# Stores of the attention's numerators and denominators: from SP's queue to ScalarE's, early in the next slot

## The chip, the cores and the metric

The kernel runs on one core of a Trainium2 chip. A core has five engines, each with its own stream of instructions that it works through in order: PE (TensorE, matrix products, with its weight loads shown as PEld), DVE (VectorE), ACT (ScalarE), POOL (GpSimd) and SP (SyncE, which here does nothing but issue DMA transfers). The engines wait for each other through semaphores. A DMA is started by an instruction on one engine's queue and then moves its data by itself. The metric is the device time of one execution in microseconds; the median of the runs is what counts.

## What is computed

The reference is one transformer layer on 4096 tokens of width 512, in 32-bit floats. The attention is linear and causal: a running state takes in one token after the other.

```python
q = elu(rope(x @ Wq.T)) + 1          # 16 heads of 128
k = elu(rope(x @ Wk.T)) + 1          # 4 heads, each used by 4 query heads
v = x @ Wv.T                          # 4 heads
state, z = state + outer(k_s, v_s), z + k_s
num = einsum('bhe,bhed->bhd', q_s, state)
den = einsum('bhe,bhe->bh', q_s, z) + EPS
attn = (num / den) @ Wo.T
x = layernorm(x + attn)
x = layernorm(x + ffn(x))             # Walsh-Hadamard transforms, 2 x 2048 inner columns, SiLU gate
```

The change touches how `num` and `den` leave the core.

## The kernel before

**Stages.** The attention comes first (about 43 to 910 us of the profiled execution), then the output product with Wo and the first layernorm, then the feed-forward part. Every factor of a product is split into a rounded high part and a remainder (`xh` and `xl`, `qh` and `ql`, `sh` and `sl`), and each product is made of three matrix products, which gives nearly full 32-bit precision.

**Blocks and slots.** The tokens are cut into `NB = 16` blocks of 256. The attention goes over them twice, since the weights of two of the four key heads fit at a time: pass 0 does key heads 0 and 1, pass 1 the heads 2 and 3. That makes 32 block steps `n`. A block step has four slots, `(g, p)` with key head `g` of the pass and half `p` of the block: 128 slots in all, one round of the loop over `slots` each. In each slot PE does 24 matmuls of a projection some slots ahead (`proj_q`), shares of the projections of keys and values of the block after (`proj_k`, `proj_v`), the transposes and sums of the running state (`nat_k`, `state`), the scores inside a chunk of 64 tokens (`scores`), and `av`, which brings all together.

**What `av` does.** For the head's half block it sums state times queries and values times scores in `ps_num` (L443), and the denominators of four query heads in `ps_den` (L444). ScalarE copies `ps_num` to the tile `num` (L447; three buffers), and the copy is stored to `num_d` in device memory (L449), 256 KB. After the second half (`p == 1`) ScalarE copies the denominators to `ds` (L452; one buffer), and two stores of 2 KB take them to `den_d` (L453 to 455). `num_d` and `den_d` are read again later: the denominators by `recip_load`, one block at a time, during the second pass and after; the numerators in the stage after, and some already in the last slots.

**The other work of the engines in a slot.** `rope` (L294 to 304) turns projections into rotated features: two copies on ScalarE to `sw`, a product on GpSimd (L296), one on VectorE (L297), a sum (L300), an exponential on ScalarE (L301), and a last step on VectorE (L304). `proj_q` splits the result into `qh` (ScalarE, L395) and `ql` (VectorE, L397). `scores` makes `A` from `ps_sc` with ScalarE (L416), VectorE (`am` L419, `A` L420) and GpSimd (L423); `ps_sc` has one buffer in PSUM.

**SP's queue.** Each DMA of the kernel is issued by `dma()` at L58, on SP. In the attention these are, besides the stores of numerators and denominators: the loads of x (`raw`, or `xh` and `xl` in the second pass, from `xs_d`), of weights, of the table of cosines (`csb`); and per block the transfers of shifted values, which lay `vhl` one token later into the tiles `vst` (three or four transfers) and `vd` (four). The state's matmul (L366) reads `vst`, and `av` reads `vd`. Sums of feed-forward weights for later (`wsum`, `was_d`) go through the same queue.

**What sets the order.** The kernel is written against a tile framework, whose planner takes the whole program and sets the order of each engine's stream from its own costs of each instruction; what is marked with `pin` keeps its place in program order. So the engines' streams are fixed before the run, and a change of one instruction's engine can reorder the rest. A tile pool with `bufs=n` hands out n buffers in turn; who takes one waits until the last use of its earlier content is over. The completion semaphores of DMAs are eight, given out in turn over all DMAs of all queues; a DMA waits until the one eight places before it has landed.

Of the kernel before, what the change touches and what calls it, by code (L numbers as in the profile page):

```python
# [43 lines left out]
def kernel(  # L44
# [5 lines left out]
    nc = tc.nc  # L50
    V, S, G, T = nc.vector, nc.scalar, nc.gpsimd, nc.tensor

    def dma(dst, src, pin=False):
        if dst.dtype == F32R:
            dst = dst.bitcast(F32)
        if src.dtype == F32R:
            src = src.bitcast(F32)
        i = nc.sync.dma_start(dst, src)  # L58
        if pin:
            tc.keep_in_program_order(i)  # L60

# [6 lines left out]
    num_d = [dram.tile([128, KVH, 512], F32, name=f"num_d{t}") for t in range(32)]  # L68
    den_d = [dram.tile([KVH, 4, 2, 64], F32, name=f"den_d{t}") for t in range(32)]
# [17 lines left out]
    def load_raw(src):  # L87
        pool, tag, nb = first.pop(0) if first else (praw, "raw", 3)
        raw = pool.tile([128, 512], F32, tag=tag, name="raw", bufs=nb)
        dma(raw, src)  # L90
        return raw
# [19 lines left out]
    def wo_raw(h, raw):  # L111
        WR[h] = raw
        dma(raw, wo[h], True)

    def wo_split(eng, *hs):
        for h in hs:
            if h < NH - 4:
                hi, lo = (wres.tile([128, 512], F32R, tag="w", name=x) for x in ("wh", "wl"))
            else:
                w = late["p"].tile([128, 2, 512], F32R, tag="wx", name="wx", bufs=4)  # L120
                hi, lo = w[:, 0], w[:, 1]
                if h == NH - 1:
                    late["p"].tile([128, 8], F32, tag="edge", name="edge", bufs=1)
            hilo(hi, lo, WR.pop(h), eng, True)
            WO[h] = (hi, lo)
# [3 lines left out]
    def recip_load(b):  # L129
        dn = pout.tile([128, 2, 16], F32, tag="dn", name="dn", bufs=2)  # L130
        for j in range(2):
            dma(dn[:, j], den_d[2 * b + j].rearrange("g h c q -> (g h c q)").rearrange("(p n) -> p n", p=128), True)
        return b, dn

    def recip(b, dn):
        pin(V.reciprocal(dn, dn))
        for j in range(2):
            dma(rec_d[2 * b + j].rearrange("(p n) -> p n", p=128), dn[:, j])
# [41 lines left out]
    with ExitStack() as es:  # L180
# [109 lines left out]
        def rope(ps, csb, f, stay=False):  # L290
            cosb = csb[:, 0:1].to_broadcast([128, 2, 256])
            sinb = csb[:, 1:2].to_broadcast([128, 2, 256])
            sw = pe.tile([128, 2, 256], F32, tag="sw", name="sw", bufs=3)
            S.activation(sw[0:64], ps[64:128], AF.Copy)  # L294
            S.activation(sw[64:128], ps[0:64], AF.Copy)  # L295
            G.tensor_tensor(sw, sw, sinb, ALU.mult)  # L296
            V.tensor_tensor(ps, ps, cosb, ALU.mult)  # L297
            yield
            x1 = ps if stay else pe.tile([128, 2, 256], F32, tag="x1", name="x1", bufs=2)
            V.scalar_tensor_tensor(x1, ps, 1.0, sw, ALU.add, ALU.add)  # L300
            S.activation(sw, x1, AF.Exp, bias=neg1)  # L301
            yield
            f = (ps if stay else sw) if f is None else f
            V.scalar_tensor_tensor(f, sw, 1.0, x1, ALU.min, ALU.max)  # L304
            return f

        def proj(n, keys):
            B = blk[n]
            ps = pmm.tile([128, 2, 256], F32, tag="mm", name="ps_qk")
            for j, key in enumerate(keys):  # L310
                i = 0
                for k in range(4):
                    for wa, xa in ((0, "xh"), (0, "xl"), (1, "xh")):
                        T.matmul(ps[:, j], W[key][wa][:, k * 128:(k + 1) * 128], B[xa][:, k],  # L314
                                 start=i == 0, stop=i == 11)
                        i += 1
            return ps
# [68 lines left out]
        def proj_q(j):  # L386
            n, g, hp = j // 4, j // 2 % 2, j % 2
            s, b = divmod(n, NB)
            B = blk[n]
            ps = proj(n, [("q", s, g, 2 * hp), ("q", s, g, 2 * hp + 1)])  # L390
            f = yield from rope(ps, B["csb"], None, hp == 1)
            if hp == 0:
                B["q", g] = tuple(p3.tile([128, 4, 256], F32R, tag=t, name=t, bufs=4) for t in ("qh", "ql"))
            qh, ql = (a[:, 2 * hp:2 * hp + 2] for a in B["q", g])
            S.activation(qh, f, AF.Copy)  # L395
            yield
            V.tensor_tensor(ql, f, qh.bitcast(F32), ALU.subtract)  # L397
# [28 lines left out]
        def av(n, g, p):  # L426
            s, b = divmod(n, NB)
            B = blk[n]
            A = B.pop(("A", g, p))
            qh, ql = B["q", g]  # L430
            sh, sl, _ = B["S"][g]
            gs = slice(g * 128, (g + 1) * 128)
            if p == 0:
                B["den", g] = pden.tile([4, 256], F32, tag="den", name="ps_den")
            den = B["den", g]
            ps = pnum.tile([128, 2, 256], F32, tag="num", name="ps_num")
            for c2 in range(2):
                c = 2 * p + c2
                t = slice(64 * c, 64 * c + 64)
                ops = [(sh[:, c], qh[:, :, t]), (sh[:, c], ql[:, :, t]), (sl[:, c], qh[:, :, t]),  # L440
                       (B["vd"][:, c, 0, gs], A[:, c2]), (B["vd"][:, c, 1, gs], A[:, c2])]
                for i, (l, r) in enumerate(ops):
                    T.matmul(ps[:, c2], l, r, start=i == 0, stop=i == len(ops) - 1)  # L443
                T.matmul(den, selr[:, c], A[:, c2], start=c == 0, stop=c == 3)  # L444
            gg = 2 * s + g
            num = p3.tile([128, 4, 2, 64], F32, tag="num", name="num", bufs=3)
            S.activation(num.rearrange("p h c q -> p c h q"),  # L447
                         ps.rearrange("p c (h q) -> p c h q", h=4), AF.Copy)
            dma(num_d[2 * b + p][:, gg], num.rearrange("p h c q -> p (h c q)"))  # L449
            if p == 1:  # L450
                ds = pout.tile([4, 256], F32, tag="ds", name="ds", bufs=1)
                S.activation(ds, den, AF.Copy, bias=EPS_DEN)  # L452
                for j in range(2):  # L453
                    dma(den_d[2 * b + j][gg].rearrange("h c q -> c h q"),
                        ds[2 * j:2 * j + 2].rearrange("c (h q) -> c h q", h=4))

        def wcomb(p):
            r = {}
# [14 lines left out]
        def wcomb_all():  # L473
            for p in range(8):
                yield from wcomb(p)
                yield
                yield
# [56 lines left out]
        def go(gen):  # L534
            if gen is not None:
                next(gen, None)
# [14 lines left out]
        for j in range(2):  # L551
            c = slice(j * 512, (j + 1) * 512)
# [9 lines left out]
        nsc = SA  # L562
        gw = wcomb_all()
        gk = gs1 = gv = None
        for i, (n, g, p) in enumerate(slots):
            nxt = n + 1 < N
            sl = (g, p)
# [11 lines left out]
                go(gk)  # L579
            if sl == (1, 0):  # L580
                go(gk)
            gq2 = proj_q(i + QA) if i + QA < NQ else None
            go(gq2)
            if sl == (0, 0):
# [40 lines left out]
            elif sl == (1, 1):  # L625
                go(gs1)
                if n == N - 2:
                    gs2 = state(N - 1, 1)
                    go(gs2)
            av(n, g, p)  # L630
            if sl == (0, 1) or n == N - 2:
                go(gv)
# [63 lines left out]
            if sl == (1, 1):  # L696
                if "dn" in cur:
                    recip(*cur.pop("dn"))
                if NB + LAG <= n < N - 4 + LAG:
                    cur["dn"] = recip_load(n - NB - LAG)  # L700
                blk.pop(n - 1, None)

        wo_split(V, 11)
        wo_split(G, 12)
# [340 lines left out]
    with ExitStack() as es:  # L1045
# [23 lines left out]
        for n in range(NS):  # L1069
            f, p = divmod(n, 8)  # L1070
            bank, sv, c = {}, {}, {}
# [13 lines left out]
            for s, tag in enumerate(SEQ):  # L1085
# [3 lines left out]
                for u in (1, 0):  # L1089
# [3 lines left out]
                    i = 0  # L1093
# [11 lines left out]
                    if s in (1, 4, 6):  # L1105
                        src, k, q = {1: (ps, 0, 0), 4: (bank.get(("b", u)), 4, 3), 6: (ps, 2, 1)}[s]
# [68 lines left out]
    with ExitStack() as es:  # L1175
# [53 lines left out]
        for idx, (n, s) in enumerate(order):  # L1229
# [40 lines left out]
            i = 0  # L1270
# [98 lines left out]
```

## Time and profile before

| what | value |
|---|---|
| median of 3 runs | 2250.24 us (2250.07 to 2251.79) |
| profiled execution, its own time | 2251.69 us |
| its span | 2250.0 us |
| granted TensorE clock, mean | 0.991 |
| PE busy over the span | 2190.9 us, 97% |
| DVE busy | 1742.0 us, 77% |
| ACT busy | 1376.5 us, 61% |
| POOL busy | 1294.6 us, 58% |
| DMA queue of SP | 501.19 MB, 69.7% of 16 engines' span |
| attention stage, 40 to 910 us: DVE, ACT busy | 761.50 and 634.49 of 870 us |

How to read it. "Busy" is the time that an engine spends on its operations; an engine that issues DMAs is not counted busy for that. Matmuls overlap in the array, so PE's busy time counts more than the time between their starts, and PE at 97% may still stand for some 2 us here and there. A wait is given as `engine line <- engine tile line: us, times, longest`: who waited, for what, in all. A line of the timeline gives start, duration, engine, operation, and in brackets how long the engine was idle just before and what ended it. The chain that ended last is followed back from the last instruction of the run, so its shares say which engine the end depended on.

### The profile page before, as it was taken

The numbers are of one execution on the slowest core, as the hardware profiler recorded it, in microseconds if no ns is written. First come the engines' busy times: TensorE is split into PE (matmuls) and PEld (weight loads), VectorE is DVE, ScalarE is ACT, GpSimd is POOL, SyncE is SP. The second block draws the span as 40 slices with busy tenths as digits, with TensorE's granted clock in tenths as the row PEclk, the third lists the DMA queues.
The fourth block names the chain that finished last, engine by engine and source line by source line (L and its number), as shares of the span: only waits on it lengthen the run. The fifth ranks groups of instructions, "written<-read, shape, count | busy, mean of one in ns | idle before, by whom it ended". The sixth has DMA issues, their size and how long they took to land.

```text
span 2250.0 us, 42158 instructions
## 1 busy us (share of the span) xinstructions
PE 2190.9 (97%) x14319; PEld 1989.9 (88%) x14319; DVE 1742.0 (77%) x2690; ACT 1376.5 (61%) x2490; POOL 1294.6 (58%) x1089
## 2 busy tenths in 40 slices
PE   8999999899999999999999999999999999999998
PEld 8999999899999998788888778778888888999998
DVE  8999998888888888688898766766866765665655
ACT  8777776677777776444443466655655655554553
POOL 5666665555555556377887446565555555533332
PEclk9999999999999999999999999999999999999999
DMA  6666665555666666889998876876766767886673
GB/s 223 204 211 197 224 218 174 164 173 181 191 199 185 199 182 198 317 264 280 296 275 276 285 262 218 249 235 193 240 211 195 244 196 213 280 287 217 228 247 128
DMA packets 360121, 503.88 MB, mean 224 GB/s; under 512 B 67964, under 2 KB 187004, under 8 KB 355938
## 3 DMA queue, kind: packets, MB, share of 16 engines
q1 hardware_dynamic: 359906, 501.19, 69.7%
q8 instruction: 113, 1.85, 0.3%
q14 instruction: 102, 0.84, 0.1%
HBM read 282.76 MB, written 156.76 MB: 195 GB/s over the span
## 4 chain that ended last, share of the span: by engine, by line
PE 62%; DVE 15%; DMA 7%; ACT 6%; issue 4%; SPq 3%; POOL 2%; DVEq 0%; POOLq 0%; ACTq 0%
PE ps_a L1096 14%; PE ps_wo L174 11%; PE ps_da L1276 8%; PE ps_b L1096 7%; PE ps_qk L314 5%; PE ps_db L1276 4%; PE ps_c L1096 3%; SPq L58 3%; DVE ps_qk L297 2%; PE ps_v L263 2%; PE ps_dc L1276 2%; PE ps_num L443 2%; DMA vst<-vhl 2%; DVE am L419 2%; DVE ql L397 1%
## 5 line engine op out<-in xcount | busy, mean ns | idle before, releaser
L314 PE MATMUL ps_qk<-xh,wh 128*128 128x256 f32 x1280 | 357.7, 279 | 1.2 <-DVE x L300 0.8
L314 PE MATMUL ps_qk<-xl,wh 128*128 128x256 f32 x1280 | 356.9, 279 | 0.0
L314 PE MATMUL ps_qk<-xh,wl 128*128 128x256 f32 x1280 | 356.7, 279 | 0.0
L1078 POOL TENSOR_TENSOR cc<-cc 128x512 f32<-128x512 f32 x96 | 146.4, 1528 | 274.9 <-ACT cc L1075 130.5
L95 DVE TENSOR_TENSOR wol<-A,woh 128x512 fp32r<-128x512 f32 x217 | 222.3, 1031 | 95.8 <-ACT woh L94 84.4
L296 POOL TENSOR_TENSOR sw<-sw,csb 128x512 f32<-128x512 f32 x160 | 212.3, 1327 | 134.7 <-ACT sw L295 118.7
L423 POOL TENSOR_SCALAR_AFFINE_SELECT A<-A 64x512 fp32r<-64x512 f32 x256 | 196.0, 766 | 144.4 <-DVE am L419 92.1
L314 PEld LDWEIGHTS ps_qk<-xh,wh 128*128 128x128 f32 x1280 | 242.3, 189 | 5.5 <-DVE ql L397 1.4
L314 PEld LDWEIGHTS ps_qk<-xl,wh 128*128 128x128 f32 x1280 | 241.2, 188 | 0.9
L314 PEld LDWEIGHTS ps_qk<-xh,wl 128*128 128x128 f32 x1280 | 241.3, 189 | 0.7
L94 ACT ACTIVATE woh<-A 128x512 fp32r<-128x512 f32 x217 | 135.1, 628 | 124.6 <-PE ps_b L1096 72.7
L94 ACT ACTIVATE hah<-hraw 128x512 fp32r<-128x512 f32 x212 | 132.1, 629 | 123.8 <-PE ps_da L1276 65.2
L95 POOL TENSOR_TENSOR hal<-hraw,hah 128x512 fp32r<-128x512 f32 x74 | 98.6, 1332 | 188.8 <-PE ps_da L1276 82.2
L1096 PE MATMUL ps_a<-yoh,woh 128*128 128x512 f32 x512 | 200.5, 393 | 5.8 <-ACT sv L1103 5.2
L1096 PE MATMUL ps_a<-yol,woh 128*128 128x512 f32 x512 | 200.1, 391 | 0.0
L1096 PE MATMUL ps_a<-yoh,wol 128*128 128x512 f32 x512 | 197.2, 391 | 0.0
L95 DVE TENSOR_TENSOR hal<-hraw,hah 128x512 fp32r<-128x512 f32 x138 | 99.0, 723 | 106.5 <-PE ps_da L1276 40.3
L1103 ACT ACTIVATE sv<-ps_a,wsc 128x512 f32<-128x512 f32 x192 | 127.0, 680 | 35.0 <-PE ps_a L1096 34.7
L174 PE MATMUL ps_wo<-wh,oh 128*128 128x512 f32 x368 | 144.5, 393 | 0.0
L174 PE MATMUL ps_wo<-wl,oh 128*128 128x512 f32 x368 | 144.0, 391 | 0.0
L174 PE MATMUL ps_wo<-wh,ol 128*128 128x512 f32 x368 | 143.9, 391 | 0.0
L297 DVE TENSOR_TENSOR ps_qk<-ps_qk,csb 128x512 f32<-128x512 f32 x160 | 111.3, 696 | 40.6 <-ACT sw L295 39.3
(306 smaller groups left out, 7312.3 us busy)
## 6 DMA issues: line engine op xcount, KB each, us to landing
hraw<-hop_d SPq DMA_DIRECT2D x224, 256.0 KB
num_d<-num SPq DMA_DIRECT2D x128, 256.0 KB
rb<-rec_d SPq DMA_DIRECT2D x128, 256.0 KB
hop_d<-hS SPq DMA_DIRECT2D x128, 256.0 KB
vd<-vhl SPq DMA_DIRECT2D x128, 252.0 KB
nt<-num_d SPq DMA_DIRECT2D x31, 1024.0 KB
A<-in_wug_dram SPq DMA_DIRECT2D x93, 256.0 KB
hop_d<-cc SPq DMA_DIRECT2D x64, 256.0 KB
```

The lines of the kernel that those rows point to most:

```text
L58: i = nc.sync.dma_start(dst, src)
L94: i = S.activation(hi, src, AF.Copy)
L95: j = eng.tensor_tensor(lo, src, hi.bitcast(F32), ALU.subtract)
L174: T.matmul(ps, l[:, h], r, start=i == 0, stop=i == 47)
L296: G.tensor_tensor(sw, sw, sinb, ALU.mult)
L297: V.tensor_tensor(ps, ps, cosb, ALU.mult)
L314: T.matmul(ps[:, j], W[key][wa][:, k * 128:(k + 1) * 128], B[xa][:, k], start=i == 0, stop=i == 11)
L423: G.affine_select(ah, ah.bitcast(F32), pattern=[[0, 8], [1, 64]], compare_op=ALU.is_ge, fill=0.0, base=0, channel_multiplier=-1)
L1078: G.tensor_tensor(x, x, c.pop(("g", q)), ALU.mult)
L1096: T.matmul(ps, w[:, u, k], y[:, k], start=first and i == 0, stop=i == 5, skip_group_check=not first)
L1103: S.activation(x, ps, AF.Copy, scale=sc)
L1276: T.matmul(pj[j], ops[qd][al][:, r, js], BW[s][bl][ip], start=first and (i == 0 or i == 3 and pj is ps), stop=i >= 45 or last and i == 23, ...
```

## The change

`dma()` gets an argument for the issuing engine. `av` no longer stores at once: it puts the store of `num`, and for the second half the two stores of `ds`, as functions on a list `puts`. The loop over the slots empties the list in the next slot, after that slot's first steps of `gq` and `gk` (a projection's and a key rope's next part) and before `proj_q` of the slot, and issues the stores on ScalarE's queue. After the last slot the list is emptied once more. 256 of the kernel's 2090 DMAs move: 128 of 256 KB and 128 of 2 KB.

```diff
-    def dma(dst, src, pin=False):
+    def dma(dst, src, pin=False, eng=nc.sync):
...
-        i = nc.sync.dma_start(dst, src)
+        i = eng.dma_start(dst, src)
...
             S.activation(num.rearrange("p h c q -> p c h q"),
                          ps.rearrange("p c (h q) -> p c h q", h=4), AF.Copy)
-            dma(num_d[2 * b + p][:, gg], num.rearrange("p h c q -> p (h c q)"))
+            puts.append(lambda: dma(num_d[2 * b + p][:, gg], num.rearrange("p h c q -> p (h c q)"), eng=S))
             if p == 1:
                 ds = pout.tile([4, 256], F32, tag="ds", name="ds", bufs=1)
                 S.activation(ds, den, AF.Copy, bias=EPS_DEN)
                 for j in range(2):
-                    dma(den_d[2 * b + j][gg].rearrange("h c q -> c h q"),
-                        ds[2 * j:2 * j + 2].rearrange("c (h q) -> c h q", h=4))
+                    puts.append(lambda j=j: dma(den_d[2 * b + j][gg].rearrange("h c q -> c h q"),
+                                                ds[2 * j:2 * j + 2].rearrange("c (h q) -> c h q", h=4), eng=S))
...
         gk = gs1 = gv = None
+        puts = []
         for i, (n, g, p) in enumerate(slots):
...
             if sl == (1, 0):
                 go(gk)
+            while puts:
+                puts.pop(0)()
             gq2 = proj_q(i + QA) if i + QA < NQ else None
...
                 blk.pop(n - 1, None)
+        while puts:
+            puts.pop(0)()
```

## The prediction

> **What bounds the kernel now.** I read the busy table first, then the attention stage alone (40 to 910 us; the changed lines run nowhere else), then what PE and SP wait for there, then single stalls. The page:
>
> ```profile
> PE 2190.9 (97%) x14319; PEld 1989.9 (88%) x14319; DVE 1742.0 (77%) x2690; ACT 1376.5 (61%) x2490; POOL 1294.6 (58%) x1089
> ...
> PE 62%; DVE 15%; DMA 7%; ACT 6%; issue 4%; SPq 3%; POOL 2%; DVEq 0%; POOLq 0%; ACTq 0%
> ...
> q1 hardware_dynamic: 359906, 501.19, 69.7%
> ```
>
> and the table by stretch (from:to and length, then busy time and count of PE, PEld, DVE, ACT and POOL, then granted clock, DMA share, GB/s):
>
> ```profile
> 40.00:910.00 870.00, 835.57 (x6967) 815.49 (x6966) 761.50 (x1222) 634.49 (x1176) 530.00 (x533) 0.98 0.61 193
> ```
>
> PE is the bound. A block of 256 tokens has 4 slots of 56 matmuls, which start 0.117 us apart when nothing is in the way, so 32 blocks need 32 x 224 x 0.117 = 839 us of the some 867 that they take. No change to queues can win more than about 28 us, and anything that makes PE pause costs in full. DVE is 88% busy beside it, ACT 73%. Next the waits of SP and PE in the stage (us in all, times, longest):
>
> ```profile
> SPq L58 <- ACT num L447: 58.6, 26, 5.9
> SPq L58 <- ACT ds L452: 25.6, 9, 6.7
> SPq L58 <- DMA xh<-xs_d: 18.6, 28, 2.0
> ```
>
> ```profile
> PE ps_sc L409 <- DVE A L420: 9.2, 3, 5.1
> PE ps_v L263 <- DVE ql L397: 8.4, 6, 4.4
> PE ps_s L366 <- DMA vst<-vhl: 7.1, 13, 1.2
> ```
>
> Two kinds of stall in them matter. The first kind recurs in blocks of the second pass: the state matmul (L366) waits for the stores of the shifted values, which SP issues among the stores of the change. SP's queue, and PE just after it:
>
> ```profile
> 607.02 0.88 SPq L58 DMA_DIRECT2D vst<-vhl  x1
> 608.00 0.48 SPq L58 DMA_DIRECT2D num_d<-num  x1
> 608.58 1.33 SPq L58 DMA_DIRECT2D den_d<-ds  x2
> 609.96 1.54 SPq L58 DMA_DIRECT2D vst<-vhl  x2
> ```
>
> ```profile
> 614.22 0.62 PE L366 MATMUL ps_s<-vst,kfn 128*128 128x256 f32 x3 [0.61 <-DMA vst<-vhl]
> ```
>
> The second is DVE's order. At 126.33 PE stands 0.98 us for a ql, because seven DVE instructions of two ropes, a state sum and the score correction stand close together:
>
> ```profile
> 126.33 0.39 PE L263 MATMUL ps_v<-wh,xh 128*128 128x256 f32 x1 [0.98 <-DVE ql L397]
> ```
>
> One stall at the end of the stage hangs on the stores as well: the num copy waits for an earlier num_d store, queued behind some 3 MB of loads, and with it the weights behind it on ACT and PE (4.83 us idle at 909.34, and half clock for some us after).
>
> ```profile
> 907.92 0.60 ACT L447 ACTIVATE num<-ps_num 128x512 f32<-128x512 f32 x1 [6.05 <-DMA num_d<-num]
> ```
>
> **The change, part by part.** The sum is made against the profiled run's own 2251.69 us (span 2250.0, 1.69 around it), 1.45 above the median of 2250.24; I add the sum to the median.
>
> *Taken from SP.* 256 issues. One num_d issue takes 425 ns at the median, one den_d issue 268 (the longest 2003 and 1459), by these rows:
>
> ```profile
> L58 SPq DMA_DIRECT2D num_d<-num x128: 319/425/2003, 43.9 to 908.5; - x128
> L58 SPq DMA_DIRECT2D den_d<-ds x128: 234/268/1459, 51.1 to 909.3; - x128
> ```
>
> At the medians that is 128 x 0.425 + 128 x 0.268 = 88.7 us; added up over the trace it is 78.2 + 49.7 = 127.9 us. SP is no bound, and its 84.2 us of waits for num and ds cost something only where a transfer behind them is late. Three such places:
> - Second pass, vst: 7.1 us over 13 waits. In the built order of the changed kernel the last vst store stands 20 to 24 matmuls before the state matmul instead of 16, 0.5 to 0.9 us more, and num_d and den_d are gone from between. Bounds 0 and -7.1; I take -5.
> - Pass change (361 to 440 us): ACT stands 3.95 us for a wv load that SP issued late, PE 4.44 us after it. The load's own landing, 4.4 us from issue, stays. Bounds 0 and -7, I take -3.
> - End of the stage: bounds +5 and -6. ACT's last stores now wait themselves for SP's 1 MB loads of numerators, but the num copy can start earlier. I take -3.
>
> Sum of gains: -11.
>
> *Added to ACT.* The same 256 issues, now between its activations, at the same duration (the nearest row, since ACT issues nothing before): 88.7 to 127.9 us on top of 634.49 of 870, from 73% to 83 to 88% busy. What hides it is ACT's 235 us idle in the stage. What is behind an issue on ACT is the rope's sw copies, exps and qh, and DVE and POOL already wait for the sw copies (38.5 us in 53 waits of DVE, 117.6 us in 79 of POOL). Bounds: 0 if all fall into idle time, +128 if all lie on the path. Between them I go by the chain that ended last: ACT has 6% of 2250 us on it, 135 of its 1376.5 busy us, so a tenth of its work counts. A tenth of 89 to 128 is 9 to 13; I take +10.
>
> *Waits that ACT now holds.* In the built program each DMA waits for the landing of the DMA eight before it, of either queue. 224 of ACT's 256 stores carry such a wait, 158 of them for a transfer of SP's; most lie 40 to 60 matmuls (5 to 7 us) behind it, and a vst transfer lands in 3.49 us in the chain of waits. SP's waits of this sort are 18.6 us for xh, and 9.2 for xl. Bounds: 0 if all have landed, +28 if ACT took them all over and on the path. A quarter of them, 7 us, at a tenth: +1. The store's wait for its own num or ds costs nothing: it is issued a slot (some 6.7 us) after the copy, num's three buffers cover a store that is one slot late, and ds, with one buffer, is written again only two slots on.
>
> *The order of all the rest.* The planner orders every engine's stream anew, and this I hold for the largest term. I counted DVE instructions per seven successive matmuls in both built programs (matmuls 400 to 7300). Places with five or more: 6 before, 40 after, with up to nine; between matmuls 400 and 3480 they are 2 before, 27 after, about two per block of the first pass; from 3481 to 7000 0 before, 9 after. A DVE instruction of these takes 0.68 us (the am row and its neighbours at 125.00: 0.67 to 0.70), so six take 4.1 us while seven matmuls need 0.8; what hides it is only what DVE runs ahead. The trace prices it: of the 11 places with four in the first pass, five held PE up by 0.79 to 1.14 us, 0.95 in the mean (a sixth by 0.57, five not). Bounds: below, 0, or -5 if these five stalls go (an order for SP's sake can also be the better one); above, 36 x 1.9 = +68 if each costs twice what a place with four does. I take 25 new ones in the first pass at 0.95 less the 4.8 lost there already, = +19, and the 9 of the second pass at half of it, as DVE has lighter stretches around them, = +4: +23, of which the +10 for ACT's issues pays for part (the same pause is not lost twice); for the overlap I take off 3.
>
> Sum: -11 + 10 + 1 + 23 - 3 = +20, so 2251.69 + 20 = 2271.7 for the profiled run, 2250.24 + 20 = 2270 for the median.
>
> One rule weighed here: the Trainium skill, DMA: Bandwidth & Descriptors, section "Issuing engines are not separate DMA queues", says that DMAs of scalar, sync and gpsimd run on the same 16 engines and interleave, so that another issuing engine saves only the time of initiating. It speaks against a gain beyond SP's issue time; the trace has all transfers at 61% of the DMA engines' time in the stage, which agrees that they are not the bound. By the rule alone the gain would be the vst share, -5, and the sum +26.
>
> **Rivals.** *Faster (2230 to 2244, middle 2238).* ACT's idle 235 us swallow the issues, the new order runs ahead of its bunches, and the gains stand: -11 to -12. For it: in the trace ACT's median instruction starts 1.5 us before the matmul that stands at its place in the built order, and 5 of 11 places with four cost nothing. Against: 27 bunches where there were 2. It decides if the mean price of a bunch is under some 0.2 us.
>
> *Within 0.2% (2246 to 2254).* 0.2% (4.5 us) is about what a measurement of this kernel can tell from no change. Gains and losses cancel, price of a bunch about 0.3 us, ACT's issues hidden.
>
> *Much slower (2286 to 2320).* An issue on ACT takes not 0.425 and 0.268 us but what SP's slow ones do when many descriptors are being made at once: vd's mean is 1.00 us. At 1.0 for num_d and 0.6 for den_d it is 205 us, ACT is 96% busy and becomes the bound beside DVE: a third of it on the path is +45 more with the order's cost, 2295 or above. Against: most of the stores stand in slots with no burst.
>
> **How the numbers follow.** Forecast (likeliest) 0.46, own range 2256 to 2286; faster 0.26; within 0.2% 0.09; much slower 0.19. So faster 0.26, same 0.09, slower 0.65. For 8 in 10 I leave out the better half of the faster case (below 2237, 0.11) and the upper part of the worst (above 2300, 0.09): 2237 to 2300. Predicted: 2270.
>
> **What would show it.** Right: num_d and den_d rows under ACT's queue at 0.3 to 0.5 us; ACT's stretch 40 to 910 at 720 to 760 us with its issues; the stage 20 us longer; "PE ps_v <- DVE ql", "PE ps_sc <- DVE A" or "PE ps_qk <- DVE" up from 20 us to 40 or more, spread over the first pass, twice a block; "PE ps_s <- DMA vst" under 3 us; the 6.05 us of the num copy gone. Wrong: if PE's waits for DVE are no longer than before, the order does not cost and the time falls to 2238; if ACT itself is what DVE and PE wait for, or its stores wait for landings, the worst case holds. Least sure is the price of a bunch, since the trace of before holds so few.

## The result and the profile after

The changed kernel takes 2350.04 us in the median of four runs (2341.46 to 2355.72) against 2250.76 us of the kernel before: a ratio of 1.0437 (95% interval 1.0399 to 1.0476), 99 us slower. The forecast was 2270 us with a range up to 2300. The direction came out as forecast, but by luck: the term that gave the forecast its sign is not the one that costs. The size did not: the loss is five times what was forecast, and the experiments below show that it comes from a term that the prediction had put at 1 us. One execution among those of the experiments, 2384.57 us at a granted clock of 0.849 in the run with the first head's stores on ACT, is left out of that run's ratio.

The page of the changed kernel's profiled execution (span 2353.0 us):

```profile
PE 2228.9 (95%) x14319; PEld 2017.0 (86%) x14319; DVE 1750.5 (74%) x2690; ACT 1371.3 (58%) x2490; POOL 1297.9 (55%) x1089
...
q1 hardware_dynamic: 340194, 467.36, 63.4%
q10 hardware_dynamic: 19712, 33.83, 4.2%
...
PE 59%; DMA 13%; DVE 10%; ACT 6%; POOL 5%; issue 4%; SPq 3%; ACTq 1%; DVEq 0%; POOLq 0%
```

A second queue, q10, now carries the stores. ACT is no busier in operations than before (its issues are not counted as busy), and in the chain that ended last it is not ACT that has grown but DMA, from 7% to 13%, and POOL, from 2% to 5%. The stage (the table by stretch, columns as before) now ends about 102 us later:

```profile
40.00:1012.00 972.00, 875.31 (x6968) 845.33 (x6966) 763.67 (x1221) 628.45 (x1174) 527.38 (x532) 0.95 0.56 172
```

The same number of matmuls as before takes 972 us in place of 870, at a granted clock of 0.95 in place of 0.98. I added up the pauses of PE from the start times of its matmuls: every interval of more than 0.35 us, less the 0.117 us of an undisturbed one. Between matmuls 400 and 2900 (first pass) they were 5.6 us before and are 37.9 now, between 3480 and 7000 (second pass) 10.6 and 51.5. Together that is 73 us more of standing; the rest of the two passes' +102 us is matmuls that start more slowly, nearly all of them within 8 us after a pause. The stages behind the attention take as long as before (1325.6 and 1325.4 us from matmul 7240 on).

PE's waits in the first 1030 us (us in all, times, longest) name ACT first:

```profile
PE ps_num L443 <- ACT num L447: 39.6, 18, 5.9
PE ps_sc L409 <- DVE A L420: 14.9, 14, 3.3
PE ps_num L443 <- ACT sh L382: 11.6, 6, 4.1
...
PE ps_s L366 <- DMA vst<-vhl: 0.9, 2, 0.7
```

The last line was 7.1 us before, and the first was this:

```profile
PE ps_num L443 <- ACT num L447: 1.0, 1, 1.0
```

So the hoped-for gain is there: the stores of the shifted values are no longer waited for. And a new wait is there that is far larger. Where it comes from is seen on ACT, here in the timeline of the changed kernel (idle time just before an instruction, and what ended it, in brackets):

```profile
245.81 0.36 ACT L452 ACTIVATE ds<-ps_den 4x256 f32<-4x256 f32 x1
250.30 0.37 ACTq L58 DMA_DIRECT2D num_d<-num  x1
251.76 0.85 ACTq L58 DMA_DIRECT2D den_d<-ds  x2
252.66 0.69 ACT L301 ACTIVATE sw<-ps_qk,neg 128x512 f32<-128x512 f32 x1 [6.49 <-DMA xs_d<-xh]
```

and on SP, DVE and PE in the same microseconds:

```profile
241.92 4.50 SPq L58 DMA_DIRECT2D wsum<-in_wug_dram  x4
246.52 0.55 SPq L58 DMA_DIRECT2D xs_d<-xh  x1
247.15 0.38 SPq L58 DMA_DIRECT2D xs_d<-xl  x1
247.59 0.49 SPq L58 DMA_DIRECT2D xs_d<-xh  x1
```

```profile
253.38 0.70 DVE L304 SCALAR_TENSOR_TENSOR ps_qk<-sw,ps_qk 128x512 f32<-128x512 f32 x1 [4.65 <-ACT sw L301]
```

```profile
257.24 0.58 PE L443 MATMUL ps_num<-qh,sh 128*128 128x256 f32 x1 [4.51 <-ACT num L447]
257.62 0.41 PE L443 MATMUL ps_num<-ql,sh 128*128 128x256 f32 x1
```

ACT is done at 246.17 and could go on with the rope. Its next instruction is the store of num, and in the built program that store waits for the transfer eight places earlier: xs_d<-xh, which SP issues only at 246.52, since it was late with the wsum loads. ACT issues its store at 250.30, 3.78 us after that, and the two small stores behind it wait for the next xs_d transfers in the same way. In all, 6.49 us without an operation on ACT. DVE gets no rope in that time (4.65 us idle), the num copy behind it is late, and PE stands 4.51 us for a free ps_num. After the pause its matmuls take 0.41 us in place of 0.28 and start 0.21 us apart.

I call the time between the end of ACT's previous instruction and the issue of a store a *stand*. In the changed kernel 58 stores stand for more than 0.3 us, 92.8 us in all (counted as in the table below; 32 of them over 1 us). In each of the 58 the store waits on one of the eight completion semaphores, the one that it will count up itself. For all but 1.2 us of this time the awaited transfer had been issued already, 3.3 to 9.7 us before the store, and had not landed; 89.3 of the 92.8 us go to transfers that SP had issued.

### The profile page after: what moved, and what is told of

The parts are those of the page before. It is cut to its first block, busy times and chain, and to the rows that moved or that the text cites. A ratio compares the mean times of both kernels' runs of the same rounds, so it can differ in the third digit from the quotient of the medians.

```text
span 2353.0 us, 42056 instructions
## 1 busy us (share of the span) xinstructions
PE 2228.9 (95%) x14319; PEld 2017.0 (86%) x14319; DVE 1750.5 (74%) x2690; ACT 1371.3 (58%) x2490; POOL 1297.9 (55%) x1089
## 4 chain that ended last, share of the span: by engine, by line
PE 59%; DMA 13%; DVE 10%; ACT 6%; POOL 5%; issue 4%; SPq 3%; ACTq 1%; DVEq 0%; POOLq 0%
PE ps_a L1101 13%; PE ps_da L1281 7%; PE ps_qk L314 7%; PE ps_b L1101 7%; PE ps_wo L174 5%; PE ps_v L263 4%; PE ps_db L1281 4%; PE ps_c L1101 3%; SPq L58 3%; PE ps_num L443 3%; DMA rb<-rec_d 2%; PE ps_dc L1281 2%; DMA yraw<-yq_d 1%; DMA vd<-vhl 1%; DMA xs_d<-xh 1%
## 5 line engine op out<-in xcount | busy, mean ns | idle before, releaser
L294 ACT ACTIVATE sw<-ps_qk 64x512 f32<-64x512 f32 x160 | 95.3, 596 | 117.2 <-PE ps_qk L314 45.0
```

## The experiments

Three theories were to be told apart. W: ACT stands at its stores for transfers that have not landed. O: the planner's new order costs, the largest term of the prediction. I: the issue time on ACT costs. To separate order from queue I fixed the order by hand: a list of one built program's order is turned into ordering edges (no semaphores) in another.

```diff
+def _force(tc):
...
+    for e, steps in want.items():
...
+            if prev is not None:
+                tc.add_manual_dep(got[e][at], prev.name, nosync, reason="order")
+            prev = got[e][at]
```

It covers all matmuls, all instructions of DVE, ACT and POOL, and SP's transfers other than the stores; the stores are placed by the planner. In the traces of the runs with a fixed order the sequences of PE, DVE, ACT, POOL and SP's other transfers are those of the kernel that gave the order, without one exception. Each ratio below is against executions of the kernel before in the same session, whose median lay between 2246.91 and 2250.67 us.

**The changed kernel's order with the stores on SP.**

```diff
-            puts.append(lambda: dma(num_d[2 * b + p][:, gg], num.rearrange("p h c q -> p (h c q)"), eng=S))
+            puts.append(lambda: dma(num_d[2 * b + p][:, gg], num.rearrange("p h c q -> p (h c q)"), eng=nc.sync))
```

(and the same for the denominators, with the changed kernel's order fixed)

> The order of the matmuls, of DVE, ACT and POOL and of SP's other transfers is that of the changed kernel, fixed by hand; the 256 stores stand one slot late, but on SP's queue. Theory W (ACT stands at its stores until an earlier transfer has landed; in the changed kernel 63 such stands of over 0.3 us, 96 us in all): no stands are left, the time falls back to 2250 to 2265 us. Theory O (the planner's new order, the term of +23 in the prediction, is what costs): the time stays at 2320 to 2350. A mixture gives the share of each.

Measured: 2263.78 us, ratio 1.007 (1.0046 to 1.0094). PE's pauses are 6.8 us in the first pass and 12.6 in the second, nearly those of before. The order that I had held for the main cost runs at almost full speed once the stores are off ACT. Theory O falls as the main cause. 14 us stay, and what they are made of is only known in part: 8.8 us of ACT's waits are for its one `ds` buffer, which the deferral on SP holds longer (below).

**The order of before with the stores on ACT**, one slot late as in the changed kernel.

> The counterpart: the order of all compute and of SP's other transfers is that of before, fixed by hand; the 256 stores stand one slot late on ACT's queue. Theory W: ACT's idle time just before its stores is 80 to 110 us in all and the time is 2320 to 2350. Theory O: the time is 2250 to 2265, and any stands of ACT lie in time that it had spare. Theory I (the issue time on ACT, some 80 us by the rows of the changed kernel, costs and not the stands): 2270 to 2290 with few stands.

Measured: 2320.65 us, ratio 1.032 (1.0298 to 1.0342); 41 stands of over 0.3 us, 75.4 us in all; PE's pauses 18.1 and 47.8 us. So most of the loss comes with the queue, in an order that is good on SP. Theory W holds, with the time at the lower end of what it gave and the stands a little under it.

Of these 75 us the second head's stores had 72: what stands between them and the first head's is the block's burst of transfers for vst and vd and what follows it on SP. This allows the sharpest test, each half of the stores alone.

**Only the first head's stores on ACT**, the order of before:

```diff
+            put = puts.append if g == 0 else lambda f: f()
+            eng = S if g == 0 else nc.sync
-            dma(num_d[2 * b + p][:, gg], num.rearrange("p h c q -> p (h c q)"))
+            put(lambda: dma(num_d[2 * b + p][:, gg], num.rearrange("p h c q -> p (h c q)"), eng=eng))
```

> Only the stores of a block's first head (g = 0) go to ACT's queue in the next slot; those of the second stay on SP as before; the order of all compute and of SP's other transfers is that of before, fixed by hand. In the run with all stores on ACT in this order, the first head's stores (64 of num and 64 of den in a pass's terms, half of the issue time) had 4 us of stands, the second head's 73 us, since these follow a block's burst of eight transfers of shifted values. Theory W (stands): within 10 us of before, 2245 to 2262, stands under 10 us. Theory I (issue time on ACT, half of some 107 us here): about half of that run's +71, 2280 to 2290.

Measured: 2251.36 us, ratio 1.0003 (0.9989 to 1.0016), 13.3 us of stands (a little over what theory W gave), 58.2 us of issue time on ACT.

**Only the second head's stores on ACT** (`g == 1` in the same lines):

> The other half: only the stores of the second head (g = 1) on ACT, the order of before. Theory W: nearly the whole loss, 2300 to 2325, with 60 us or more of stands. Theory I: as the first half, 2280 to 2290.

Measured: 2348.84 us, ratio 1.0443 (1.0395 to 1.0491), 81.7 us of stands with only 40.6 us of issue time. The time is above what theory W gave (2300 to 2325) and far above theory I. Half of the stores cost nothing, the other half cost as much as the whole change. The half with more issue time on ACT is the free one. Lines of ACT in this run, each just behind one or more stands, which are part of its idle time:

```profile
608.21 0.59 ACT L297 ACTIVATE sw<-ps_qk 64x512 f32<-64x512 f32 x1 [1.91 <-DMA vd<-vhl]
611.67 0.63 ACT L398 ACTIVATE qh<-sw 128x512 fp32r<-128x512 f32 x1 [2.27 <-DMA wsum<-in_wug_dram]
641.44 0.59 ACT L297 ACTIVATE sw<-ps_qk 64x512 f32<-64x512 f32 x1 [4.62 <-DMA den_d<-ds]
```

These two also settle theory O's measure, which was a count of places with five or more DVE instructions within seven matmuls: the kernel before had 6 such places; with each engine's order the same as there, the built program of the free half has 62, that of the dear half 22. So the count is no property of an engine's order, and it does not foretell the time. Why the second half alone loses 28 us more than both halves together is not settled; its stands are 6 us longer in all, and its second pass has 14 us more of pauses.

**The issue time alone.** The stores stay on SP as before; ACT gets 256 small copies of some 0.41 us in their places, which write to a tile that nobody reads.

```diff
+        def spend():
+            i = S.activation(junk, ones4[:, 0:1].to_broadcast([128, 256]), AF.Copy)
...
+            puts.append(spend)
```

> The stores stay on SP as before; in their places early in the next slot ACT gets 256 small copies of a constant into a tile that nobody reads, some 0.4 us each, about the 105 us that the issues take it in the changed kernel, and they wait for nothing. The order of all else is that of before. Theory W: under +15, 2250 to 2265. Theory I: 2290 to 2320.

Measured: 2267.62 us, ratio 1.0084 (1.0061 to 1.0108). That is 3 us above what theory W gave, but it was not the dose I meant: since a copy of a constant waits for nothing, the planner put all 256 ahead, between 5.0 and 347.7 us. So I repeated it with copies that read the slot's `num` and can't be moved ahead.

```diff
-            i = S.activation(junk, ones4[:, 0:1].to_broadcast([128, 256]), AF.Copy)
+            i = S.activation(junk, num.rearrange("p h c q -> p (h c q)")[:, 0:256], AF.Copy)
```

> As the run with 256 small copies on ACT, but each copy reads the slot's num tile, so that it can't be moved ahead: in the other run the planner had put all of them into the first 348 us. In the built program they stand evenly through the stage, 256 x some 0.41 us = 105 us, as much as the changed kernel's issues take, and wait for no transfer. Order of all else as before. Theory W: 2250 to 2268. Theory I: 2290 to 2320.

Measured: 2255.73 us, ratio 1.0028 (1.0013 to 1.0043), some 6 us. The copies' row of that run, and its stage:

```profile
L432 ACT ACTIVATE junk<-num x256: 399/408/428, 45.2 to 916.0; 128x256 bf16<-128x256 f32 x128
```

```profile
40.00:920.00 880.00, 838.90 (x6985) 816.20 (x6984) 763.35 (x1227) 719.71 (x1436) 532.47 (x535) 0.99 0.60 191
```

ACT is 82% busy here and PE hardly notices. 104 us of ACT's time, about the 105 us that the changed kernel's issues take it, cost some 6 us if nothing waits in them. Theory I is bounded by that.

**A queue without the shared semaphores.** The changed kernel with `eng=G`, POOL's queue:

> As the changed kernel, but the stores are issued on POOL's queue, whose transfers have completion semaphores of their own, so that in the built program not one of the 256 stores waits for a transfer's landing. Theory W: 2245 to 2275, since POOL is only 61% busy in the stage. Theory O: the planner bunches here too (15 places with five DVE instructions in seven matmuls, against 6 and 40), so about a quarter of the loss, 2270 to 2285. If an issue on a computing engine costs in itself: 2290 or more.

Measured: 2272.22 us, ratio 1.0107 (1.0078 to 1.0136). The issues are dearer than on ACT, as the rows of this run show, and yet 78 us of the loss are gone:

```profile
L58 POOL DMA_DIRECT2D num_d<-num x128: 570/611/744, 45.6 to 925.9; - x128
L58 POOL DMA_DIRECT2D den_d<-ds x128: 567/576/593, 51.9 to 927.0; - x128
```

The expectation is wrong in one point. POOL's transfers have eight semaphores of their own, but they too go round, apart from the set that SP and ACT share: in the built program 248 of the 256 stores wait for POOL's store eight places earlier. What differs is the age of the awaited transfer. Here it was issued 15 to 42 us before the store (27 at the median). For a store on ACT in the changed kernel the transfer eight places earlier was 8.1 us old at the median, and 162 of 256 times under 10 us. No wait of POOL for its stores ends with a landing. The time alone does not tell theory W from theory O, whose ranges overlap here, and the planner's order is another again. The pauses of the two passes (16.6 us, 16.2 before) are those of before; what is lost lies mostly in the pass change (101.1 us for matmuls 2900 to 3480, 88.9 before) and at the stage's end (55.4 against 50.2), and was not followed further.

**The two parts of the change apart.** Deferred, but on SP:

> Only the deferral: the stores are issued early in the next slot, but on SP's queue; the planner orders as it likes. Theories W and I: as before, 2243 to 2255. If the deferral itself costs (num and ds are held longer, SP's later loads come later): 2260 or more.

Measured: 2268.6 us, ratio 1.0091 (1.0068 to 1.0114). The deferral is not free. ACT's waits in this run:

```profile
ACT ds L452 <- DMA den_d<-ds: 36.2, 15, 3.6
```

`ds` has one buffer. With the two small stores a slot later, and behind other transfers on SP, the next copy to ds comes too soon. (In the changed kernel, with the stores on ACT, this wait is 1.2 us.) So the next run defers the numerators alone:

```diff
-                    puts.append(lambda j=j: dma(den_d[2 * b + j][gg].rearrange("h c q -> c h q"),
-                                                ds[2 * j:2 * j + 2].rearrange("c (h q) -> c h q", h=4), eng=S))
+                    dma(den_d[2 * b + j][gg].rearrange("h c q -> c h q"),
+                                                ds[2 * j:2 * j + 2].rearrange("c (h q) -> c h q", h=4))
```

(with the numerators' store on SP)

> On SP's queue, only the numerators' stores wait for the next slot; the denominators are stored at once. All stores deferred on SP cost +18.6 us, with 36.2 us in which ACT's next copy to ds (one buffer) waited for the late store of the one before. If that buffer is what deferral costs: 2247 to 2256. If holding num back costs, or SP's later issue: 2262 or more.

Measured: 2238.05 us, ratio 0.9955 (0.9941 to 0.9968). This beats both kernels, by about 10 us against before (a later run of the same idea, below, by 7), and it is faster than either branch of the expectation. SP's queue at the place shown in the prediction:

```profile
604.19 0.89 SPq L58 DMA_DIRECT2D vst<-vhl  x1
605.18 1.08 SPq L58 DMA_DIRECT2D den_d<-ds  x2
606.31 1.54 SPq L58 DMA_DIRECT2D vst<-vhl  x2
607.89 4.45 SPq L58 DMA_DIRECT2D vd<-vhl  x4
612.39 1.01 SPq L58 DMA_DIRECT2D num_d<-num  x1
```

The numerators' store now stands behind the transfers for vst and vd in place of among them (the denominators' stores are still between), and PE's wait for vst falls from 7.1 us:

```profile
PE ps_s L366 <- DMA vst<-vhl: 3.5, 7, 0.9
```

Is that the place on SP or the planner's new order? The same with the order of before fixed:

> Only the numerators' stores wait for the next slot, on SP, with the order of all compute and of SP's other transfers as before, fixed by hand. The run without a fixed order was 11.7 us faster than before, most of it in the second pass (414.9 us for its matmuls 3480 to 7000 in place of 421.9). If the store's place on SP (behind the stores of the shifted values that PE waits for) is what won it: 2236 to 2244. If the planner's new order won it: 2247 to 2254.

Measured: 2243.68 us, ratio 0.9969 (0.9957 to 0.9981). The second pass takes 413.0 us for its matmuls 3480 to 7000, against 421.9 before and 414.9 with the free order. So the place alone wins the second pass, and PE's wait for vst does not occur there any more. Whether the free order adds anything is not shown: the intervals of the two ratios overlap, and the two profiled executions took 2243.71 us (free) and 2243.19 (fixed).

At once, but on ACT:

```diff
-            dma(num_d[2 * b + p][:, gg], num.rearrange("p h c q -> p (h c q)"))
+            dma(num_d[2 * b + p][:, gg], num.rearrange("p h c q -> p (h c q)"), eng=S)
```

(and the same for the denominators)

> The other part of the change alone: the stores go to ACT's queue, but at once, as before, not in the next slot; the planner orders. Theory W: the stands stay, since an issue waits for the transfer eight places earlier wherever it is put: 2300 to 2370. If the place in the next slot is what makes them stand: 2250 to 2280.

Measured: 2343.15 us, ratio 1.0418 (1.0362 to 1.0473); 58 stands, 84.8 us. The queue costs with and without the deferral.

**A mixture that missed.** Numerators deferred, the first head's on ACT and the second's on SP; denominators at once on SP; the planner free to order.

```diff
+            puts.append(lambda: dma(num_d[2 * b + p][:, gg], num.rearrange("p h c q -> p (h c q)"), eng=S if g == 0 else nc.sync))
```

> The numerators' stores wait for the next slot, those of the first head on ACT's queue and those of the second on SP's; the denominators are stored at once on SP. Theory W: 64 of the changed kernel's 128 numerator stores move to ACT, the ones that hardly stand, so the time is that of the deferral on SP alone, 2233 to 2245. Theory I (issue time on ACT): 64 issues at 0.35 us are 22 us more on ACT, 2245 to 2260.

Measured: 2260.01 us, ratio 1.0036 (1.0021 to 1.0051). I had expected the first head's stores to be free here as they were in the fixed order. They are not: 13 of the 64 stand, each over 1 us, 31.1 us in all, 17.0 of them for a den_d transfer that SP had issued 3.4 to 5.8 us before. The number eight places earlier is another transfer when the order is another. So my forecast from theory W missed, and the trace shows stands where I had expected none: a kernel's stands have to be looked up anew in each built program.

The kernels side by side, sorted by stands. PE's pauses are those of matmuls 400 to 2900 and 3480 to 7000 together; stands are those over 0.3 us; issue time is the sum of ACT's issue instructions, or of the engine named.

| stores | order | stands: number, us | issue time on ACT, us | PE's pauses, us | median, us | ratio |
|---|---|---|---|---|---|---|
| at once on SP (before) | before | none | 0 | 16.2 | 2250.76 | 1 |
| num deferred on SP | planner | none | 0 | 10.0 | 2238.05 | 0.9955 |
| num deferred on SP | before | none | 0 | 7.8 | 2243.68 | 0.9969 |
| all deferred on SP | changed | none | 0 | 19.4 | 2263.78 | 1.0070 |
| all deferred on SP | planner | none | 0 | 27.5 | 2268.60 | 1.0091 |
| all deferred on POOL | planner | none | 151.3 (POOL) | 16.6 | 2272.22 | 1.0107 |
| at once on SP, 256 copies on ACT, early | before | none | 104 (copies) | 28.3 | 2267.62 | 1.0084 |
| at once on SP, 256 placed copies on ACT | before | none | 104 (copies) | 19.3 | 2255.73 | 1.0028 |
| first head on ACT | before | 12, 13.3 | 58.2 | 14.6 | 2251.36 | 1.0003 |
| first head's num on ACT | planner | 13, 31.1 | 20.9 | 30.5 | 2260.01 | 1.0036 |
| all deferred on ACT | before | 41, 75.4 | 107.3 | 65.9 | 2320.65 | 1.0320 |
| second head on ACT | before | 53, 81.7 | 40.6 | 77.8 | 2348.84 | 1.0443 |
| all at once on ACT | planner | 58, 84.8 | 112.4 | 78.5 | 2343.15 | 1.0418 |
| all deferred on ACT (the change) | changed | 58, 92.8 | 105.3 | 89.4 | 2350.04 | 1.0437 |

From 31 us of stands on, time and pauses go with the stands, though not in proportion: 13.3 us of them cost nothing, 31.1 some 8 us, 75 to 93 some 70 to 100. The issue time does not go with the loss (58.2 us of it free, 40.6 with the largest loss). Among the kernels without stands the losses are of up to 1.1%, from the `ds` buffer, from the copies put early, and from causes not followed.

## Why the prediction was wrong, by its own steps

**Waits that ACT now holds: +1, between 0 and +28.** This is the step that failed. The mechanism was named, with the right count of 224 stores and a distance (5 to 7 us) near the measured one. Three things in its price were wrong. The upper bound of 28 came from two rows of SP's waits (18.6 and 9.2 us); all rows of SP's waits for transfers in the stage before add up to 52 us, and the 256 stores on ACT waited longer than that, since they are put among SP's transfers, 52 of the 58 standing ones those of the second head, behind the block's burst. It is not that the awaited transfer was younger: the transfer eight places before had been issued 8.1 us before at the median for a store on ACT, and 7.8 us for SP's issues before. The landing was taken as 3.49 us, one of those in the chain, which also has an xh<-xs_d of 5.99 us; the stands show transfers that were 3.3 to 9.7 us old when the store could go, and a few that were issued only after ACT had come to its store. And a tenth of the wait was counted, as for ACT's ordinary work. The placed copies, 0.41 us each, cost about that (6 of 104 us); the stands, up to several us in a row, cost nearly their whole sum. That single short delays fall into slack and long ones do not is my reading of these two. Measured: 92.8 us of stands in place of 28 at most, and +71 us on the time where only queue and place were changed and the order was kept, in place of +1.

**The order of all the rest: +23.** Wrong as well, and held for the largest term. The changed kernel's order on SP pauses 3 us more than before in the two passes, and its whole loss, the deferral's part included, is 14 us. The count of DVE instructions per seven matmuls does not measure an engine's order: it went from 6 to 62 and 22 with the order of every engine unchanged, so it depends on how the planner lines the engines up against each other, which the run does not follow. Without this term and its overlap the sum would have been 0. That the total came out with the right sign rests on it, and is luck.

**Added to ACT: +10.** About right, as far as copies can stand for issues: the placed copies cost 6 us (3 to 10 by the interval) for 104 us. The row taken from SP was near: on ACT an issue of num_d takes 349 ns at the median in place of 425, one of den_d 279 in place of 268.

```profile
L58 ACTq DMA_DIRECT2D num_d<-num x128: 332/349/378, 44.1 to 1009.6; - x128
L58 ACTq DMA_DIRECT2D den_d<-ds x128: 243/279/1857, 51.3 to 1011.5; - x128
```

**Taken from SP: -11.** The vst share was right (7.1 us down to 0.9, -5 forecast). The other two were not: matmuls 2900 to 3480 at the pass change take 88.2 us in place of 88.9 (-3 forecast), and 7000 to 7240 at the stage's end 52.0 in place of 50.2 (-3 forecast, +5 as bound).

**The store's wait for its own num or ds costs nothing, with one `ds` buffer.** On ACT the buffer held: 1.2 us of ACT's waits in the changed kernel are for it. It would not have on SP: 36.2 us in the run with all stores deferred there, which is 30 us slower than the one that defers num alone.

**The rival "much slower"** had the right sign and the wrong mechanism: at the median issues are hardly slower on ACT than on SP (0.349 and 0.279 us, not 1.0 and 0.6). Its range of 2286 to 2320 did not hold the time either. One sign of being wrong that the prediction named was the right one: that ACT's stores wait for landings. That is what the profile shows.

## What to carry to other kernels

A DMA issued on ACT stopped all that was behind it on ACT until the transfer that its instruction waits for had landed, and that was mostly one of another queue: look up in the built program which transfer each moved issue waits for, how old it will be, and whether it lies in a burst. Do not price such stands by the engine's share of the path: here 31 us of them cost some 8 us, and 75 to 93 us nearly the whole. Before a queue is changed, try the place on the old queue: here the numerators' stores behind the burst on SP won about what the change was to win (ratios 0.9955 and 0.9969 for the forecast gains of 11 us) and added nothing to ACT. Where a planner orders the streams, fix the order by hand in an experiment before the order is blamed.

## What the runs showed of the hardware that was not expected

An issue of the same 256 KB store took 349 ns at the median on ACT, never over 378, 425 ns on SP with up to 2003, and 611 ns on POOL. A small den_d store took 279, 268 and 576 ns. And pauses of PE went with more loss than themselves: in the stage of the changed kernel the granted clock is 0.95 against 0.98, and after the 4.51 us pause shown above the matmuls started 0.21 us apart in place of 0.117, in a stretch of 6.8 us for which the profile has half the clock.
